# A mixture-of-experts router with its tokens on partitions, the centroid products as eight more columns of its weight, and the squared norm on ScalarE

## The chip, the cores and the metric

The kernel runs on one core of a Trainium2 chip. The metric is the device time of one execution in microseconds (us), and the median of several runs stands for a kernel. TensorE (PE in the profile) multiplies matrices, VectorE (DVE), ScalarE (ACT) and GpSimd (POOL) work element by element, SyncE (SP) issues most transfers. Each engine works through its own instructions in order and waits on semaphores where it needs another engine's result. Matrix products land in PSUM, everything else lives in SBUF.

## The reference, cut to what matters

Two layers, each an attention block and a feed-forward block, on x of 8 batches x 112 tokens x 256 features, with a context of 375 rows per batch, all in fp32:

```python
x = x + xattn0(layernorm(x), ctx)      # 16 heads of 16, 375 keys
x = x + moe(layernorm(x))              # 8 experts, the nearest 2 per token, hidden 1024
x = x + xattn1(layernorm(x), ctx, mask)
x = x + ffn1(layernorm(x))             # quantized linear, conv over tokens, silu, linear
```

The change is in the router of `moe`, which finds the two nearest of eight centroids c by a hyperbolic distance:

```python
xh   = project(x @ Wp + bp)            # project: x * min(1, 0.95 / |x|)
cp   = project(centroids)              # 8 x 256
xn   = min(sum(xh * xh), 0.99);  cn = min(sum(cp * cp), 0.99)
dot  = einsum("bnd,ed->bne", xh, cp)
diff = max(xn + cn - 2 * dot, 0)
dist = arccosh(max(1 + 2 * diff / ((1 - xn) * (1 - cn) + 1e-7), 1 + 1e-7))
top_v, top_i = top_k(-dist, 2);  weights = softmax(top_v)
```

So of the mapped token `y = x @ Wp + bp` the router needs just nine numbers: its squared norm and its product with each of the eight projected centroids. The factor min(1, 0.95/|y|) is applied to these afterwards.

## The kernel before, in words

**Attention of layer 0, 0 to about 280 us.** It goes by blocks of one batch b (112 tokens). A plan holds tuples (slot, place, step); the steps are issued in the order of slot and place, so work of several batches is interleaved by hand, and each engine keeps that order apart from what the program's scheduler moves where no dependence holds it. Batch b has slots 4b to 4b+12:

- `norm` and `query` (slots 4b-5, 4b-3): layer norm, turned by TensorE (t_n), then the q products (t_q, L534) of 16 instructions;
- `key` in two halves (t_k, L229; 8 instructions of 375 columns each) and `value` (t_v, L236; on DVE three additions put the bias onto v), both ahead of their use;
- `scores` for group g of four heads (slot 4b+g, place 0): four products (sc, L584) into two tiles, of which DVE takes the negative maximum of each row (top, L587), two instructions per group, 64 in layer 0;
- `lower` (slot 4b+4): turns the maxima (t_top, L603) and adds them to q (qa, L607);
- `turned` (slots 4b+5 to 4b+8): the scores again, with keys on partitions (t_p, L617), and exp on ACT (L629);
- `weighted` (one slot after): the products with v, collected in po (L639);
- `finish_o`, `finish_t`, `project` (slots 4b+10 to 4b+12): po copied by ACT, turned (t_o), divided by the sum of exp on DVE (o), turned again (t_oT), multiplied with the output weight (t_out), added to x, and the layer norm's statistics of the result on DVE.

PSUM is short: t_k, t_v, sc and t_p share three tiles of two banks ("pair"), and all of t_n, t_q, t_top, t_o, t_oT, t_out, t_rn, t_xh share one single bank (`misc`, buffer "m"). po has a bank, and behind its 448 columns the same bank has four slots of 16 columns (`small`) for the router's little products; the profile names these after the bank, so a router product is shown as `po`.

**The router.** `route(b, i)` has slot 4b+13+i, after the attention of its batch, so its steps lie between the steps of the next batches:

- step 0, `norm` and `turn`: rn on DVE, two transposes (t_rn, L288), a copy on ACT (rnT, L290), 128 features x 112 tokens twice;
- step 1, `hyper`: eight products t_xh (L297) with the features of the result on partitions, then four activations on ACT that add the bias: xh (L304) and its square xsq (L305), for each half of the features;
- step 2, `centre`: products with the centroids (L313, 8 columns) and of xsq with ones (L315, 1 column), which bring the tokens onto partitions; DVE copies the nine numbers (g, L317), clamps the squared norm (cx, L259) and works out 0.95/|y| by a bit trick and three Newton steps of tiny operations;
- step 3, `distance`: 11 operations of 112x1 or 112x8 on DVE;
- steps 4 and 5, `pick`: the two nearest, 9 small DVE operations and one sum;
- step 6, `place` (place 5 of its slot, the other steps 7): products with a lower triangle and ones count how many tokens came before (L364, L366); DVE reads the rank (row, L368) and forms row numbers (rf, at, L373); two indirect transfers on POOL (L375) scatter rn to the experts' lists in DRAM (`tok`). rn has two buffers, so rn of block b+2 waits for both scatters of block b;
- step 7, `weigh`: the two weights, on DVE.

`centroids()` (slot -1, place 7) projects the centroids once: a product with ones, and ten or so small DVE operations giving cproj, cn and cn1. In slots 8 to 19, at place 5, lie twelve steps that turn layer 1's two feed-forward weights into ternary values on DVE: `ternary` (absolute sums, L446, 1.2 us each, and others).

**From 297 us on.** Behind the last scatter, `further` works out which 13 further tiles of 128 tokens the experts need, then the experts' 21 tiles run (t_h L799, t_y L810), to about 520 us; layer 1 follows.

**Loads.** At the start SP issues x, the context, then the router's weight wp (L119), then w1T and w2T (1 MB each) for `ternary`, then the masks and zeros for the scratch in DRAM. ACT's queue issues the columns of biases, wq, wk, wv, `rows` (two biases of 256 values, broadcast to all partitions, L100) and wo.

Of the kernel before, what the change touches and what calls it, by code (L numbers as in the profile page):

```python
# [24 lines left out]
E, F = 8, 1024  # L25
# [29 lines left out]
def xattn_ffn_kernel(  # L55
# [190 lines left out]
    class Router:  # L246
        def __init__(self, pool, misc, small):
# [2 lines left out]
            self.cn = const([128, E], "cn")  # L250
            self.cn1 = const([128, E], "cn1")

        def tmp(self, name, n, p=S):
            return self.pool.tile([p, n], F32, tag=f"r_{name}", name=name)

# [7 lines left out]
        def centroids(self):  # L263

            cent = col("cent", 0, 2 * E).rearrange("p (c e) -> p c e", c=2)
            csq = self.pool.tile([128, 2, E], F32, tag="r_csq", name="csq")
            nc.vector.tensor_mul(csq, cent, cent)
            t = self.small("t_c")[:, :E]
            for c in range(2):
                nc.tensor.matmul(t, ones, csq[:, c, :], start=(c == 0), stop=(c == 1))  # L270
            nc.vector.tensor_copy(self.cn, t)
            cs = self.tmp("cs", E, 128)
            self.ball_scale(self.cn, cs, E, "c")
            nc.vector.tensor_mul(self.cproj, cent, cs.unsqueeze(1).to_broadcast([128, 2, E]))
            nc.vector.tensor_mul(self.cn, self.cn, cs)
            nc.vector.tensor_mul(self.cn, self.cn, cs)
            nc.vector.tensor_scalar_min(self.cn, self.cn, 0.99)
            nc.vector.tensor_scalar(self.cn1, self.cn, -1.0, 1.0, ALU.mult, ALU.add)

        def norm(self, b, stats):  # L280
            n = self.pool.tile([S, D], F32, tag="r_n", name="rn")
# [9 lines left out]
            return nT  # L291

        def hyper(self, nT):
            t = self.misc("t_xh")[:, : 2 * S].rearrange("p (c s) -> p c s", c=2)
            for o in range(2):
                for c in range(2):
                    nc.tensor.matmul(  # L297
                        t[:, o, :], wp_t[:, c, o * 128 : (o + 1) * 128], nT[:, c, :],
                        start=(c == 0), stop=(c == 1),
                    )  # L300
            xh = self.pool.tile([128, 2, S], F32, tag="r_xh", name="xh")
            xsq = self.pool.tile([128, 2, S], F32, tag="r_xsq", name="xsq")
            for o in range(2):
                nc.scalar.activation(xh[:, o, :], t[:, o, :], AF.Identity, bias=col("bp", o))  # L304
                nc.scalar.activation(xsq[:, o, :], t[:, o, :], AF.Square, bias=col("bp", o))  # L305
            return xh, xsq

        def centre(self, xh, xsq):

            tmp = self.tmp  # L310
            t = self.small("t_g")[:S, : E + 1]
            for c in range(2):
                nc.tensor.matmul(t[:, 0:E], xh[:, c, :], self.cproj[:, c, :], start=(c == 0), stop=(c == 1))  # L313
            for c in range(2):
                nc.tensor.matmul(t[:, E : E + 1], xsq[:, c, :], ones[:, 0:1], start=(c == 0), stop=(c == 1))  # L315
            g, r = tmp("g", E + 1), tmp("r", 1)
            nc.vector.tensor_copy(g, t)  # L317
            self.ball_scale(g[:, E : E + 1], r, 1, "x")
            return g, r

        def distance(self, g, r):

            tmp = self.tmp
            xn = tmp("xn", 1)
            nc.vector.scalar_tensor_tensor(xn, g[:, E : E + 1], r, r, ALU.mult, ALU.mult)
# [7 lines left out]
            nc.vector.scalar_tensor_tensor(dif, g[:, 0:E], m2r, self.cn[:S], ALU.mult, ALU.add)  # L333
# [145 lines left out]
    def attention(layer, stats, stats_next):  # L479
        scale = (0.25, 0.0625)[layer]  # L480
        res = None
        with (
# [219 lines left out]
            if layer == 0:  # L702
                rt = Router(ap, misc, small)
                rs = [{} for _ in range(B)]

                def route(b, step):
                    r = rs[b]
                    if step == 0:
                        r["n"] = rt.norm(b, stats_next.pop(b))
                        r["nT"] = rt.turn(r["n"])  # L710
                    elif step == 1:
                        r["x"] = rt.hyper(r.pop("nT"))
                    elif step == 2:
                        r["g"] = rt.centre(*r.pop("x"))
# [12 lines left out]
                add(-1, 7, rt.centroids)  # L727
                for i, step in enumerate(ternary(small)):
                    add(8 + i, 5, step)
                for b in range(B):  # L730
                    for i in range(8):
                        add(4 * b + 13 + i, 5 if i == 6 else 7, route, b, i)
                last = 4 * (B - 1)
                add(last - 2, 9, load_layer1, "kvq")
                add(last + 12, 9, load_layer1, "o")
                for b, ns in enumerate(((3, 6, 9), (15, 16, 17))):
                    add(last + ns[0], 4, key, 1, b, 0)
                    add(last + ns[1], 4, key, 1, b, 1)
                    add(last + ns[2], 4, value, 1, b)
# [288 lines left out]
```

## Time and the profile before

| | us |
|---|---|
| median of five runs | 793.2 |
| the five runs | 791.57, 792.49, 793.2, 793.35, 798.0 |
| the profiled execution, its own time | 793.08 |
| its span in the trace | 791.4 |

The profile is of that one execution; the span is what lies between its first and its last recorded instruction. Over the span TensorE is busy 672.4 us (85%), DVE 461.3 (58%), ACT 240.7 (30%), POOL 43.2 (5%), and the mean granted TensorE clock is 0.84 of full speed. By stretches of the run:

| stretch, us | what runs | PE busy | DVE busy | ACT busy | PE clock |
|---|---|---|---|---|---|
| 0 to 25 | loads, norms, centroids | 14.34 | 19.92 | 4.06 | 1.00 |
| 25 to 95 | attention of layer 0, no router yet | 68.19 | 45.55 | 20.31 | 0.95 |
| 95 to 265 | attention with the router between | 158.33 | 105.79 | 55.84 | 0.86 |
| 265 to 297 | the last blocks and the router's tail | 15.00 | 22.78 | 4.41 | 0.74 |
| 297 to 520 | experts | 211.52 | 61.78 | 73.17 | 0.89 |
| 520 to 791 | layer 1 | 205.03 | 205.52 | 82.88 | 0.76 |

In a line of the timeline the columns are: start (us), busy time, engine, line, operation, output<-inputs, tile (partitions x elements), and how many neighbouring instructions are put together; a bracket at the end gives how long the engine had waited just before, and for what. A matrix product's tile is shown as rows*columns of the weight and then rows x columns of its output. The router's t_xh of blocks 0 to 7 starts at 106.07, 133.84, 164.91, about 194.9, 217.87, 249.50, 266.81 and 276.36 us.

### The profile page before, as it was taken

The page shows a single profiled execution, that of the slowest core. Times are in us where ns is not written, and L with a number is a line of the kernel's source. Part 1 is how long each engine was busy: PE and PEld are TensorE (multiplying, and loading weights), DVE is VectorE, ACT ScalarE, POOL GpSimd, SP SyncE. Part 2 cuts the span into 40 slices and gives each one's busy share as a digit, 9 for nine tenths or more (in the row PEclk, how much of TensorE's full clock was granted, in tenths as well). Part 3 has the DMA queues.
Part 4 walks back from the last instruction along what each step waited for, and adds up shares of the span by engine and source line. Part 5 has one row for each costly group of instructions (what it writes and reads, how often), then busy time and mean ns, then how long its engine had stood idle before and what let it go on. Part 6 is the DMA issues. An engine that isn't in the chain of part 4 may idle for free.

```text
span 791.4 us, 15060 instructions
## 1 busy us (share of the span) xinstructions
PE 672.4 (85%) x5906; PEld 483.9 (61%) x5906; DVE 461.3 (58%) x1664; ACT 240.7 (30%) x476; POOL 43.2 (5%) x83
## 2 busy tenths in 40 slices
PE   4999998999999819999999959999999999845143
PEld 2666666666666518999999845666666656621033
DVE  8845667756834761111111048758987785469975
ACT  1124343224233204334343310223334322317300
POOL 4000000100000110000000061000000000000000
PEclk9999999789777959999999985579999975556558
DMA  9999101002000014987999420000000000000001
GB/s 302 368 345 329 62 2 54 14 13 68 14 13 7 32 35 176 343 316 282 357 344 358 185 75 26 1 2 1 3 1 2 2 2 1 1 1 0 0 11 35
DMA packets 37074, 82.73 MB, mean 105 GB/s; under 512 B 3228, under 2 KB 29196, under 8 KB 31628
## 3 DMA queue, kind: packets, MB, share of 16 engines
q1 hardware_dynamic: 34092, 76.25, 27.0%
q0 software_dynamic: 1536, 3.67, 1.5%
q10 hardware_dynamic: 1376, 1.87, 0.8%
q8 instruction: 46, 0.75, 0.4%
q14 instruction: 24, 0.20, 0.1%
HBM read 61.59 MB, written 20.19 MB: 103 GB/s over the span
## 4 chain that ended last, share of the span: by engine, by line
PE 70%; DVE 17%; DMA 5%; issue 4%; ACT 2%; SPq 0%; POOL 0%; ACTq 0%; DVEq 0%; POOLq 0%
PE t_k L229 11%; PE t_h L799 10%; PE t_y L810 9%; PE t_p L617 8%; PE sc L584 8%; PE po L639 6%; PE t_q L534 4%; PE t_v L236 4%; DMA tok<-rn,at 2%; PE t_out L672 2%; DVE am L924 2%; PE t_o L651 1%; DVE top L587 1%; PE t_y L942 1%; DVE y L913 1%
## 5 line engine op out<-in xcount | busy, mean ns | idle before, releaser
L229 PE MATMUL t_k<-ctx,wk 128*128 128x375 f32 x256 | 103.1, 550 | 4.3 <-DMA ctx<-in_ctxT_dram 3.5
L584 PE MATMUL sc<-k,q 16*112 16x375 f32 x512 | 87.7, 587 | 4.9 <-DVE pT L627 2.8
L799 PE MATMUL t_h<-tnT,we 128*128 128x128 f32 x672 | 91.5, 280 | 0.1
L799 PEld LDWEIGHTS t_h<-tnT,we 128*128 128x128 f32 x672 | 87.3, 193 | 6.5 <-ACT hT L803 1.6
L803 ACT ACTIVATE hT<-t_h,we 128x128 f32<-128x128 f32 x168 | 61.4, 367 | 90.7 <-PE t_h L799 85.1
L617 PE MATMUL t_p<-qa,k 17*125 17x112 f32 x1536 | 81.8, 324 | 2.3 <-DVE top L587 1.5
L810 PE MATMUL t_y<-we,hT 128*128 128x256 f32 x336 | 82.8, 380 | 0.0
L629 ACT ACTIVATE pT<-pT 125x672 f32<-125x672 f32 x64 | 48.8, 763 | 108.1 <-DVE pT L627 106.0
L617 PEld LDWEIGHTS t_p<-qa,k 17*125 17x125 f32 x1536 | 65.0, 217 | 21.2 <-issue 14.6
L229 PEld LDWEIGHTS t_k<-ctx,wk 128*128 128x128 f32 x256 | 52.2, 215 | 38.4 <-issue 11.5
L587 DVE TENSOR_REDUCE top<-sc 112x2 f32<-112x750 f32 x64 | 57.9, 934 | 27.8 <-PE sc L584 27.8
L627 DVE TENSOR_TENSOR pT<-t_p,maskT 125x336 f32<-125x336 f32 x128 | 56.6, 500 | 25.3 <-PE t_p L617 25.3
L639 PE MATMUL po<-pT,v 125*32 125x112 f32 x1536 | 66.3, 301 | 5.9 <-ACT pT L629 3.7
L629 ACT ACTIVATE pT<-t_p 125x672 f32<-125x672 f32 x64 | 43.3, 728 | 90.1 <-PE t_p L617 90.1
L594 DVE CUSTOM_DVE_ANT_0 sm<-sc,mask 112x375 f32<-112x375 f32 x128 | 63.0, 542 | 9.8 <-PE sc L584 9.7
L639 PEld LDWEIGHTS po<-pT,v 125*32 125x32 f32 x1536 | 43.9, 125 | 31.8 <-ACT pT L629 13.2
L810 PEld LDWEIGHTS t_y<-we,hT 128*128 128x128 f32 x336 | 59.1, 191 | 5.5
L788 DVE COPY tnT<-t_tn 128x256 f32<-128x256 f32 x21 | 8.9, 425 | 76.5 <-PE t_tn L786 70.2
L812 DVE TENSOR_TENSOR y<-t_y,we 128x256 f32<-128x256 f32 x21 | 8.9, 425 | 68.9 <-PE t_y L810 68.9
L584 PEld LDWEIGHTS sc<-k,q 16*112 16x112 f32 x512 | 29.4, 190 | 31.0 <-issue 18.9
L236 PE MATMUL t_v<-wv,ctx 128*125 128x256 f32 x192 | 45.9, 387 | 0.3 <-ACT k L557 0.3
L236 PEld LDWEIGHTS t_v<-wv,ctx 128*125 128x125 f32 x192 | 34.7, 187 | 7.4 <-ACT k L557 0.9
(207 smaller groups left out, 779.4 us busy)
## 6 DMA issues: line engine op xcount, KB each, us to landing
we<-in_WB_dram SPq DMA_DIRECT2D x21, 1152.0 KB, 8.0
we<-in_WA_dram SPq DMA_DIRECT2D x21, 1028.0 KB, 6.3
tok<-zero SPq DMA_DIRECT2D x8, 896.0 KB, 9.8
ysc<-zero SPq DMA_DIRECT2D x8, 896.0 KB, 11.1
ctx<-in_ctxT_dram SPq DMA_DIRECT2D x8, 375.0 KB, 7.6
tn<-tok SPq DMA_DIRECT2D x21, 128.0 KB, 7.0
ysc<-y SPq DMA_DIRECT2D x21, 128.0 KB, 3.2
we<-in_w1T_dram SPq DMA_DIRECT2D x1, 1024.0 KB, 9.0
```

What stands on the lines that cost most here:

```text
L229: nc.tensor.matmul(t, wts[layer]["k"][:, c, g * 128 : (g + 1) * 128], ctx_t[b][:, c, :], start=(c == 0), stop=(c == 1),)
L236: nc.tensor.matmul(t, ctx_t[b][:, c, i * KC : (i + 1) * KC], wts[layer]["v"][:, c, :], start=(c == 0), stop=(c == 1),)
L584: nc.tensor.matmul(ts[j // 2][:S, j % 2, :SK], q[r, g, :], k[r, g, :], start=True, stop=True)
L587: nc.vector.tensor_reduce(top[:, g, 2 * m : 2 * m + 2, A : A + 1], ts[m][:S, :, :SK], AX.X, ALU.max, negate=True,)
L594: nc.vector.tensor_tensor_reduce(out=sm, in0=ts[m][:S, i, :SK], in1=mask_t, scale=-1.0, scalar=3.0e38, op0=ALU.add, op1=ALU.min, accum_out ...
L617: nc.tensor.matmul(ts[j // 2][:KC, j % 2, c * S : (c + 1) * S], k[r, g, c * KC : (c + 1) * KC], qa[r, g, :], start=True, stop=True,)
L627: nc.vector.tensor_tensor(pT[:, i, :], src[:, i, :], maskT_t, ALU.add)
L629: nc.scalar.activation(pT, src, AF.Exp)
L639: nc.tensor.matmul(po[32 * j : 32 * j + 32, g, :], v[:, c, 4 * g + j, :], pTs[j // 2][:, j % 2, c * S : (c + 1) * S], start=(c == 0), stop ...
L799: nc.tensor.matmul(ph[:, i, :], w1[:, c, f * 128 : (f + 1) * 128], nt[:, c, :], start=(c == 0), stop=(c == 1),)
L803: nc.scalar.activation(hT[:, f, :], ph[:, i, :], AF.Gelu, bias=b1[:, f : f + 1])
L810: nc.tensor.matmul(py, hT[:, f, :], w2[:, f, :], start=(f == 0), stop=(f == NF - 1))
```

## The change

The mapped token is now made with the tokens on partitions: rnT is the stationary operand and the weight the moving one, so that t_xh is 112 tokens x 264 columns, 256 features and eight more columns that are the products with the projected centroids. It takes two products, issued as four instructions for fp32, instead of eight. DVE adds the bias row (256 values and eight more), ACT squares the 256 features and sums them along the row in the same instruction (`accum_out`). The products with the centroids and with ones, the four activations and the copy g are gone; `distance` reads the eight products from the new tile x, and cx reads the sum that ACT left.

For this `centroids()` multiplies Wp and the bias with the projected centroids once: four transposes of Wp, two copies by ACT, a broadcast copy of the bias, six products (twelve instructions), three copies by DVE. SP issues one transfer more, the bias row broadcast to 128 partitions (128 KB), right after wp; the input `rows` is longer by these 256 values. The steps' slots and places are the same as before.

```diff
     rowt = const([128, 2 * D], "rows")
-    nc.scalar.dma_start(out=rowt, in_=rows.partition_broadcast(128))
+    nc.scalar.dma_start(out=rowt, in_=rows[: 2 * D].partition_broadcast(128))
...
-    wp_t = load_w(wp, "wp", nc.sync)
+    wpc, bpc = const([128, 2, D + E], "wpc"), const([128, D + E], "bpc")
+    nc.sync.dma_start(out=wpc[:, :, :D], in_=wp.rearrange("(c p) n -> p c n", p=128))
+    nc.sync.dma_start(out=bpc[:, :D], in_=rows[2 * D :].partition_broadcast(128))
...
         def centroids(self):
...
+            wt = self.pool.tile([128, 2, D], F32, tag="r_wt", name="wpT")
+            for o in range(2):
+                t = self.misc("t_wp")[:, :D]
+                for c in range(2):
+                    nc.tensor.transpose(
+                        t[:, c * 128 : (c + 1) * 128], self.wpc[:, c, o * 128 : (o + 1) * 128], ident
+                    )
+                nc.scalar.copy(wt[:, o, :], t)
+            bw = self.pool.tile([128, 2, 128], F32, tag="r_bw", name="bpw")
+            nc.vector.tensor_copy(bw, col("bp", 0, 2).unsqueeze(2).to_broadcast([128, 2, 128]))
+            for k in range(3):
+                t = self.small("t_wc")[:, :E]
+                for o in range(2):
+                    lhs = wt[:, o, k * 128 : (k + 1) * 128] if k < 2 else bw[:, o, :]
+                    nc.tensor.matmul(t, lhs, self.cproj[:, o, :], start=(o == 0), stop=(o == 1))
+                nc.vector.tensor_copy(self.wpc[:, k, D:] if k < 2 else self.bpc[:, D:], t)
...
         def hyper(self, nT):
-            t = self.misc("t_xh")[:, : 2 * S].rearrange("p (c s) -> p c s", c=2)
-            for o in range(2):
-                for c in range(2):
-                    nc.tensor.matmul(
-                        t[:, o, :], wp_t[:, c, o * 128 : (o + 1) * 128], nT[:, c, :],
-                        start=(c == 0), stop=(c == 1),
-                    )
-            xh = self.pool.tile([128, 2, S], F32, tag="r_xh", name="xh")
-            xsq = self.pool.tile([128, 2, S], F32, tag="r_xsq", name="xsq")
-            for o in range(2):
-                nc.scalar.activation(xh[:, o, :], t[:, o, :], AF.Identity, bias=col("bp", o))
-                nc.scalar.activation(xsq[:, o, :], t[:, o, :], AF.Square, bias=col("bp", o))
-            return xh, xsq
-
-        def centre(self, xh, xsq):
-
-            tmp = self.tmp
-            t = self.small("t_g")[:S, : E + 1]
+
+            t = self.misc("t_xh")[:S, : D + E]
             for c in range(2):
-                nc.tensor.matmul(t[:, 0:E], xh[:, c, :], self.cproj[:, c, :], start=(c == 0), stop=(c == 1))
-            for c in range(2):
-                nc.tensor.matmul(t[:, E : E + 1], xsq[:, c, :], ones[:, 0:1], start=(c == 0), stop=(c == 1))
-            g, r = tmp("g", E + 1), tmp("r", 1)
-            nc.vector.tensor_copy(g, t)
-            self.ball_scale(g[:, E : E + 1], r, 1, "x")
-            return g, r
-
-        def distance(self, g, r):
+                nc.tensor.matmul(t, nT[:, c, :], self.wpc[:, c, :], start=(c == 0), stop=(c == 1))
+            x = self.pool.tile([S, D + E], F32, tag="r_x", name="xh")
+            nc.vector.tensor_tensor(x, t, self.bpc[:S], ALU.add)
+            return x
+
+        def centre(self, x):
+
+            g, r, sq = self.tmp("g", 1), self.tmp("r", 1), self.tmp("xsq", D)
+            nc.scalar.activation(sq, x[:, 0:D], AF.Square, accum_out=g)
+            self.ball_scale(g, r, 1, "x")
+            return x[:, D : D + E], g, r
```

More of the change, by code (lines that the diff above doesn't have):

```diff
@@ L251, in __init__ @@
             self.cn1 = const([128, E], "cn1")
+            self.wpc, self.bpc = wpc, bpc
         def tmp(self, name, n, p=S):
@@ L293, in hyper, with distance @@
         def hyper(self, nT):
[L294 to L321 removed]
+            t = self.misc("t_xh")[:S, : D + E]
+            for c in range(2):
+                nc.tensor.matmul(t, nT[:, c, :], self.wpc[:, c, :], start=(c == 0), stop=(c == 1))
[7 more added lines that the diff above has]
+            return x[:, D : D + E], g, r
+        def distance(self, dot, g, r):
             tmp = self.tmp
             xn = tmp("xn", 1)
[L325 removed]
+            nc.vector.scalar_tensor_tensor(xn, g, r, r, ALU.mult, ALU.mult)
             nc.vector.tensor_scalar_min(xn, xn, 0.99)
@@ L332, in distance @@
             dif = tmp("dif", E)
-            nc.vector.scalar_tensor_tensor(dif, g[:, 0:E], m2r, self.cn[:S], ALU.mult, ALU.add)
+            nc.vector.scalar_tensor_tensor(dif, dot, m2r, self.cn[:S], ALU.mult, ALU.add)
             nc.vector.tensor_scalar(dif, dif, xn, 0.0, ALU.add, ALU.max)
@@ L713, in route @@
                     elif step == 2:
-                        r["g"] = rt.centre(*r.pop("x"))
+                        r["g"] = rt.centre(r.pop("x"))
                     elif step == 3:
@@ L989 @@
         ),
-        "rows": np.concatenate([i["L0_xattn_b_kv"][D:], i["L0_xattn_b_out"]]),
+        "rows": np.concatenate([i["L0_xattn_b_kv"][D:], i["L0_xattn_b_out"], i["L0_ffn_bp"]]),
         "wq0": apart(i["L0_xattn_w_q"]),
```

## The prediction

> **What bounds the kernel now.** I read the page first: the chain of work that ended last, and the clock row of the 40 slices.
>
> ```profile
> PEclk9999999789777959999999985579999975556558
> ...
> PE 70%; DVE 17%; DMA 5%; issue 4%; ACT 2%; SPq 0%; POOL 0%; ACTq 0%; DVEq 0%; POOLq 0%
> ```
>
> TensorE holds 70% of the chain, and its clock falls in the eighth to thirteenth slice (139 to 257 us, 7 to 9 tenths), where the router runs. The change lies before 300 us; the router's results gate the experts there, so what it moves in that stretch passes on to the end. Next I read the timeline around block 1's router steps.
>
> ```profile
> 133.84 1.04 PE L297 MATMUL t_xh<-rnT,wp 128*128 128x112 f32 x8
> 134.91 0.35 ACT L304 ACTIVATE xh<-t_xh,cols 128x112 f32<-128x112 f32 x1 [2.25 <-PE t_xh L297]
> ...
> 135.74 1.79 DVE L587 TENSOR_REDUCE top<-sc 112x2 f32<-112x750 f32 x2 [0.62 <-PE sc L584]
> 136.06 0.41 PE L663 MATMUL t_oT<-ident,o 112*128 112x112 f32 x2 [0.35 <-ACT xsq L305]
> ...
> 139.31 0.56 PE L313 MATMUL po<-cproj,xh 128*112 128x8 f32 x4
> 139.72 0.53 PE L315 MATMUL po<-ones,xsq 128*112 128x1 f32 x4
> 140.18 1.60 PE L584 MATMUL sc<-k,q 16*112 16x375 f32 x6
> ...
> 146.52 4.72 PE L229 MATMUL t_k<-ctx,wk 128*128 128x375 f32 x8
> ...
> 151.67 0.62 DVE L607 TENSOR_TENSOR qa<-t_top,q 128x448 f32<-128x448 f32 x1 [0.91 <-PE t_top L603]
> ...
> 153.10 2.04 PE L534 MATMUL t_q<-nT,wq 128*128 128x112 f32 x16
> ```
>
> To see there: L313 and L315 hold TensorE for 0.87 us (139.31 to 140.18) though they stream 8 columns and 1; xsq (L305) holds the one "m" buffer, so t_oT waits 0.35; and qa waits 0.91 for TensorE, so in this block TensorE is the late one. In block 0, at full clock, it was the other way: TensorE waited 2.21 us up to 121.05 for DVE. Windows of 1 us show why: the clock is 1.00 in 139 to 140, 0.61 in 140 to 141, 0.50 to 150, 0.77 in 150 to 151. It was half from 140.2 to 150.5, and likewise 170.9 to 177.8, 201.7 to 205.1, 211.9 to 229.0 and 239.2 to 249.4. Last I read the late blocks and the tail.
>
> ```profile
> 231.30 0.16 DVE L373 CAST at<-rf 112x2 int32<-112x2 f32 x1
> ...
> 237.93 0.41 DVE L217 TENSOR_SCALAR rn<-x,mv,rs 112x256 f32<-112x256 f32 x1 [1.30 <-DMA tok<-rn,at]
> ```
>
> ```profile
> 275.46 0.41 PE L288 MATMUL t_rn<-ident,rn 112*128 112x112 f32 x2
> 276.36 1.15 PE L297 MATMUL t_xh<-rnT,wp 128*128 128x112 f32 x8 [0.49 <-ACT rnT L290]
> ...
> 280.40 0.15 DVE L259 TENSOR_SCALAR cx<-g 112x1 f32<-112x1 f32 x1
> ```
>
> From 230 us on, a block's two scatters (from 231.30 on, behind at) gate the rn of the block two later, whose buffer they still read. Block 7's chain is serial from t_rn to the end of layer 0.
>
> **The change, part by part.** The order is that of the changed kernel's instructions on each engine, the durations are the trace's.
>
> *Prices per block.* t_xh: 8 instructions of 112 columns, 0.97 us apart (133.84 to 134.81), become 4 of 264; t_v streams 256 in 0.23 (12 in 2.79), so 0.95: nothing gained. L313 and L315 go: -0.87 at full clock, 1.3 at half (170.58 to 171.87). ACT loses four activations, 0.35 each and 0.25 apart (1.1 us, from 134.91 to 136.00), and gains a Square of 256 elements. Its summed output no row shows; ends are the 224-element copy (0.35) and the 672-element exponential (0.73), I take 0.45, near the first by size. DVE loses the copy g (0.17) and gains an add of 112x264 out of PSUM; L571's 125x256 took 0.42, so 0.43. DVE's first clamp (cx) now waits for ACT's Square, behind the add.
>
> The Trainium skill, "ScalarE: Activation LUTs" (What ACT_TABLE_LOAD costs), gives 186 ns + 0.833 ns an element for an ACTIVATE without pointer operands: 0.40 for this Square, an estimate. By it the sum below would be 0.2 lower; no run here shows the summed output.
>
> *Start: +2.2.* centroids() gains four transposes, two ACT copies, six products and four DVE copies, and SP a transfer of 128 KB. wp was issued at 14.99 and took 6.9 us (21.9); its first reader comes after t_n (24.19 to 24.55), so 3 us cover it. The extra transfer moves w1T and w2T back one place each on SP: w1T goes at 16.11, not 15.40, and lands near 25.2 (9.0 us). On DVE the first L446 sum (1.21) now stands ahead of the first maximum, which before began at 25.77: the sum runs 25.8 to 27.0, the maximum to 27.9, the copy of the first new column to 28.0. The second pair of products waits for that copy (same PSUM bank), so TensorE, in order, has t_k's rest only then: 28.1 + 0.4 (products) + 1.35 (half of t_k) + 0.4 + 0.65, then both scores 0.75: t_q at 31.75 against 29.55. Later waits up to 95 us are on DVE and ACT (1.2 us in all), none on a transfer, so the 2.2 passes on. Bounds: 0 if the gaps take it, 3.5 if every copy adds its own wait.
>
> *Blocks 0 to 3: -3.2.* Block 1 replayed at full clock. v adds end at 135.13, add 135.56, Square 136.08, cx 136.25, the two maxima end at 137.1 and 138.25 (before 136.65 and 137.53). t_oT starts 0.35 earlier, but t_p's second half waits for the first maximum and gives it back. Next, 16 serial small operations of norm and distance (0.2 to 0.25 each by the tail's rows: 3.0 us) run before the rank's row read, which now is at 141.2; po waits for that read. Eleven more (1.6 us) stand before the next maximum: it ends at 143.85, the second at 145.0, and t_k starts at 145.05. Without L313 and L315 the scores were ready at 139.25, so this wait is the new one: behind it in DVE's queue are x, the layer norm and qa, and t_p, t_k and t_top on TensorE. The old order at full clock gives t_k at 143.5. But the old order then has 46 small operations before qa, 6.8 us from x (143.96 to 150.75), the new 35, 4.45 us: t_q waits for qa, at 150.1 new against 150.45 old, so -0.4 for block 0. In the half-clock blocks TensorE is last: t_k at 145.0 instead of 146.52, and t_q 0.9 earlier (block 1), 1.0 (block 2, t_k 176.15 instead of 178.01, then qa late), 0.9 taken for block 3.
>
> *Blocks 4 to 7 and the tail: -2.5.* at (231.30) no longer waits for g (231.22): -0.4, and rn with it, since two scatters take 6.6 us from at to rn; at 254.85 waited the same way from rf's end 254.21: -0.5. Between t_rn of block 6 and x of block 7, L313, L315 and the waits for xh and xsq (0.40, 0.24) go and the wait for the add comes: -1.1. From t_rn(7) to cx took 4.94; new: t_xh ends 1.97 after t_rn, add 0.53, Square 0.55, then the v copy (0.95) that now stands between, 4.4: -0.5.
>
> Sum: 2.2 - 3.2 - 2.5 = -3.5. The profiled execution took 793.08 (its span and 1.7 us around it), 0.1 under the median of 793.2: 789.6.
>
> The clock is a rule to weigh. The trace lost it at 140.2 with TensorE never idle, in a stretch of thin products (po, t_p, L364, L313, L315), and kept it through 119 to 121, when TensorE was idle. The Trainium skill, "TensorE: Matmul & The Clock Gate" (The HAM clock gate), has the gate fall after an idle window of about 3.4 us. The stretches agree with windows of 3.4 (10.2, 6.8, 3.4, 17.1, 10.2 us long), the idleness does not. By the page's rule the change, which opens no such gap, would leave the clock, and the sum, as they are.
>
> **Rivals.**
> - *The clock stays up in blocks 1 to 3.* For: thin products leave the windows that lost it. Against: the waits before t_k lengthen a stretch without wide products from 8.7 to 10.3 us. Then t_xh to t_q takes 16.25 everywhere, against 19.26, 18.12 and some 17.7: -3.0 - 1.9 - 1.5 - 0.4 = -6.8 in place of -3.2: 786.0.
> - *The blocks gain nothing*, DVE being the bound and the cx wait costing what qa's shorter queue gives. For: 121.05, where TensorE waited for DVE. Against: qa's 0.91 wait in block 1. 2.2 - 2.5: 792.8.
> - *Slower: the 28 operations put between the maxima hold t_k, and it is not given back.* Place: row read and second maximum, t_k 1.55 later in each of four blocks. It decides once qa is ready before TensorE comes to t_q. For: qa waited for TensorE at 151.67. Against: at half clock old t_k was later still (146.52). 2.2 + 6.2 - 2.5: 799.0.
>
> **How the numbers follow.** Forecast 0.40 (its own range 787.5 to 791.5), clock 0.14, no gain 0.20, slower 0.26: block 0 shows DVE already the late engine at full clock, and three of the four early blocks are only in part at half. The range leaves out the lower half of the clock case (786.0, so from 785.0, as some of it will keep a window) and the slower case from above its value of 799.0, so to 799.5, together 0.2. It takes in 789.6 with eight Squares at their upper bound (8 x 0.28 = 2.2) and the start at 3.5. Half a per cent, about what a measurement of this kernel can tell from no change, is at 789.2 and 797.2: faster is the clock case and over half of the forecast, 0.37; same the rest and no gain, 0.37; slower 0.26.
>
> **What would show it.** No t_g products; 32 t_xh instructions near 0.45 to 0.5 us; Square near 0.45; the second t_q near 31.75 instead of 29.55; cx behind Square; x of a block later than its second maximum, qa some 4.5 us after x; t_rn(7) to cx 4.4. Half-clock windows counted from 95 to 265 us (47.7 us now) decide between forecast and clock case; t_k starts against t_q starts decide the slower one. The prediction is wrong if the clock's stretches move by more than one window of 3.4 us, or if Square takes over 0.73.

## The result, and the profile after

The changed kernel takes 796.75 us in the median, the kernel before 794.34 over the runs taken beside it: a ratio of 1.0029, with a 95% interval of 1.0018 to 1.0039. It is 2.3 us slower (1.4 to 3.1), where 3.5 less was forecast. The range of 785.0 to 799.5 holds the time; the direction was wrong.

The profiled execution took 793.79 (span 792.1), 3.0 under the median of its kernel; that of before took 793.08, 1.3 under its own. So the two traces are only 0.7 apart, and what follows from them is where the time moved; the 2.3 comes from the timed runs. The page of the changed kernel has, as answers to the lines shown of before:

```profile
span 792.1 us, 14880 instructions
...
PEclk9999998999767958999999985579999985556558
...
PE 66%; DVE 18%; DMA 8%; issue 4%; ACT 2%; SPq 1%; POOL 0%; DVEq 0%; POOLq 0%; ACTq 0%
```

The clock falls as often as before, but elsewhere: the seventh slice (119 to 139 us) has 8 instead of 9, the twelfth 6 instead of 7, and the eighth and ninth 9 instead of 7 and 8. TensorE's share of the chain is lower (66%, 70 before), DVE's and the transfers' higher. Following the same work through both traces:

| from, to | before | after | difference |
|---|---|---|---|
| start to t_xh of block 0 | 106.07 | 110.36 | +4.29 |
| t_xh of block 0 to t_xh of block 1 | 27.77 | 30.83 | +3.06 |
| blocks 1 to 2, 2 to 3, 3 to 4 | 31.07, 29.93, 23.03 | 28.55, 27.97, 24.75 | -2.52, -1.96, +1.72 |
| t_xh of block 4 to cx of block 7 | 62.53 | 57.66 | -4.87 |
| cx of block 7 to the first t_h | 17.86 | 17.61 | -0.25 |
| first t_h to the end of the span | 493.1 | 494.3 | +1.2 |

One thing has to be taken off the first row: the first t_q, which runs before anything that the fold (the products of Wp and the bias with the centroids) adds on TensorE, starts at 18.49 instead of 19.81, and in the experiments anywhere from 18.58 to 20.73. Counted from it, t_xh of block 0 is 5.6 later, not 4.3.

Up to the experts the changed kernel is 0.5 ahead in this execution. The 1.2 behind them lie in no line that the change touches; the page has t_h waiting 1.1 for an expert's weights, and none such before.

**The start.** TensorE's timeline of the kernel before, up to the second t_q (columns as before):

```profile
24.47 0.90 PE L584 MATMUL sc<-k,q 16*112 16x375 f32 x8
25.64 2.76 PE L229 MATMUL t_k<-ctx,wk 128*128 128x375 f32 x8 [0.27 <-PE sc L584]
28.33 1.29 PE L584 MATMUL sc<-k,q 16*112 16x375 f32 x8
29.55 2.04 PE L534 MATMUL t_q<-nT,wq 128*128 128x112 f32 x16
```

The same of the changed kernel, from 23.36 to the last scores ahead of the second t_q, which starts at 33.90:

```profile
23.36 0.88 PE L592 MATMUL sc<-k,q 16*112 16x375 f32 x2
24.17 0.44 PE L287 MATMUL t_wp<-ident,wpc 128*128 128x128 f32 x2
24.54 0.88 PE L592 MATMUL sc<-k,q 16*112 16x375 f32 x2
25.35 0.44 PE L287 MATMUL t_wp<-ident,wpc 128*128 128x128 f32 x2
25.63 0.29 PE L297 MATMUL po<-cproj,wpT 128*128 128x8 f32 x2
25.84 0.88 PE L592 MATMUL sc<-k,q 16*112 16x375 f32 x2
26.65 0.39 PE L297 MATMUL po<-cproj,wpT 128*128 128x8 f32 x2
26.97 0.88 PE L592 MATMUL sc<-k,q 16*112 16x375 f32 x2
27.78 1.15 PE L231 MATMUL t_k<-ctx,wk 128*128 128x375 f32 x2
...
33.07 0.90 PE L592 MATMUL sc<-k,q 16*112 16x375 f32 x8
```

A group of scores is four heads of two instructions, each on 16 of the array's 128 rows. In one piece the eight take 0.83 us (33.07 to the t_q at 33.90): the heads run at once. Here the fold's transposes and products stand between the heads, and each head takes 0.81 by itself, so that from 23.36 to 27.78 pass 4.42 us, against 1.17 before (24.47 to 25.64): 3.24 for the four heads, 1.18 for the fold's instructions between them. The Trainium skill, "TensorE: Matmul & The Clock Gate" (Part 3: Packing small matmuls — row/col tiling), says that products on different strips of 32 rows overlap in the array; both traces agree for heads that are neighbours in the instruction stream. With instructions of the full array between them, the lines above show no such overlap.

TensorE did not wait for the fold's copies here: it is busy in all 14.00 us from 20 to 34, and on DVE each of the three copies waits for its product (0.50, 0.79 and 1.53).

And the clock fell behind this thin stretch, though TensorE had work in it all the time. Two stretches of the kernel before (columns: window, its length, busy time and instructions of PE, PEld, DVE, ACT and POOL, then the granted clock, the DMA share and GB/s), and the same two of the changed kernel:

```profile
28.00:33.00 5.00, 5.00 (x31) 3.39 (x30) 5.00 (x6) 1.04 (x2) 0.00 (x0) 1.00 1.08 378
118.00:130.00 12.00, 9.53 (x113) 6.18 (x116) 11.48 (x42) 3.69 (x8) 0.00 (x0) 1.00 0.14 43
```

```profile
28.00:33.00 5.00, 5.00 (x16) 3.14 (x15) 2.67 (x5) 0.00 (x0) 0.00 (x0) 0.66 1.07 370
118.00:130.00 12.00, 9.92 (x75) 6.38 (x76) 10.25 (x54) 2.87 (x5) 0.72 (x1) 0.72 0.01 3
```

From 29.43 the t_k instructions are 0.63 apart instead of 0.31. The changed kernel and the four kernels below that have the heads apart all show their first half clock at 28 to 31 us; of the kernel before and the eight others below none shows half clock ahead of 41 us.

**Block 0.** Two lines of TensorE's timeline in block 0 of the kernel before:

```profile
114.67 2.79 PE L229 MATMUL t_k<-ctx,wk 128*128 128x375 f32 x8
121.05 0.78 PE L639 MATMUL po<-pT,v 125*32 125x112 f32 x24 [2.21 <-DVE w1mean L455]
```

The timeline of DVE, ACT and TensorE in block 0's router of the changed kernel:

```profile
111.57 0.42 DVE L319 TENSOR_TENSOR xh<-t_xh,bpc 112x264 f32<-112x264 f32 x1
112.02 0.42 ACT L325 ACTIVATE xsq<-xh 112x256 f32<-112x256 f32 x1 [2.84 <-DVE xh L319]
112.34 0.19 ACT L325 ACTIVATION_READ_ACCUMULATOR xsq<-xh 112x1 f32 x1
112.56 0.15 DVE L263 TENSOR_SCALAR cx<-g 112x1 f32<-112x1 f32 x1 [0.58 <-ACT xsq L325]
...
117.86 0.47 PE L625 MATMUL t_p<-qa,k 17*125 17x112 f32 x4
...
119.42 0.93 DVE L595 TENSOR_REDUCE top<-sc 112x2 f32<-112x750 f32 x1
...
120.41 1.59 PE L625 MATMUL t_p<-qa,k 17*125 17x112 f32 x20 [2.08 <-DVE top L595]
...
121.93 5.37 PE L231 MATMUL t_k<-ctx,wk 128*128 128x375 f32 x8
```

The Square costs what was taken for it (0.42; 0.45 taken), with a second ACT instruction of 0.19 behind it that reads the sum. The new wait is further down: DVE works through norm, distance and the first pick before it takes the maximum at 119.42. t_p waits 2.08 for that, and the t_k behind it runs at half clock, 5.37 instead of 2.79. That the wait brought the half clock is not shown: the kernel before waited 2.21 up to 121.05, and its clock stayed at 1.00 from 118 to 130.

The early blocks as a whole follow the clock. Its mean over blocks 0 to 3 (from t_xh to the next t_xh) was 1.00, 0.84, 0.89 and 0.80 before, and is 0.89, 0.94, 1.00 and 0.73 now. If what is missing to 1.00 is lost time (an estimate; where TensorE waits it costs nothing), that makes +3.4, -3.3, -3.3 and +2.1 us, close to the measured +3.06, -2.52, -1.96 and +1.72. Without it blocks 0 to 3 gain nothing. Blocks 4 to 7 gain their 4.87 at the same clock, 0.83 before and 0.82 now.

**The tail** got better, as forecast. From t_rn of block 7 to its cx passed 4.94 before, now 3.99:

```profile
276.13 0.41 PE L308 MATMUL t_rn<-ident,rn 112*128 112x112 f32 x2 [0.27 <-DVE rn L219]
...
277.04 1.15 PE L317 MATMUL t_xh<-wpc,rnT 128*112 128x264 f32 x4
...
280.12 0.14 DVE L263 TENSOR_SCALAR cx<-g 112x1 f32<-112x1 f32 x1
```

### The profile page after: what moved, and what is told of

The parts are those of the page before. It is cut to its first block, busy times and chain, and to the rows that moved or that the text cites. A ratio compares the mean times of both kernels' runs of the same rounds, so it can differ in the third digit from the quotient of the medians.

```text
span 792.1 us, 14880 instructions
## 1 busy us (share of the span) xinstructions
PE 668.5 (84%) x5826; PEld 476.7 (60%) x5826; DVE 463.4 (59%) x1668; ACT 236.9 (30%) x462; POOL 43.2 (5%) x83
## 4 chain that ended last, share of the span: by engine, by line
PE 66%; DVE 18%; DMA 8%; issue 4%; ACT 2%; SPq 1%; POOL 0%; DVEq 0%; POOLq 0%; ACTq 0%
PE t_k L231 11%; PE t_h L807 9%; PE t_y L818 8%; PE t_p L625 8%; PE sc L592 7%; PE po L647 6%; PE t_q L542 5%; PE t_v L238 4%; DMA tok<-rn,at 4%; DMA we<-in_WA_dram 2%; DVE top L595 2%; DVE am L932 2%; PE t_out L680 2%; PE t_o L659 1%; PE t_y L950 1%
## 5 line engine op out<-in xcount | busy, mean ns | idle before, releaser
L625 PE MATMUL t_p<-qa,k 17*125 17x112 f32 x1536 | 84.7, 324 | 7.7 <-DVE top L595 5.5
L625 PEld LDWEIGHTS t_p<-qa,k 17*125 17x125 f32 x1536 | 66.7, 215 | 27.1 <-issue 14.1
```

The costliest lines, as they stand in the source:

```text
L625: nc.tensor.matmul(ts[j // 2][:KC, j % 2, c * S : (c + 1) * S], k[r, g, c * KC : (c + 1) * KC], qa[r, g, :], start=True, stop=True,)
```

## The experiments

Ratios are to the kernel before, run beside it on the same chip, with 95% intervals; absolute times differ by some us from chip to chip. Line numbers in a fence are those of that kernel.

### The two halves of the change, each by itself

The fold alone, in the kernel before:

```diff
-    wp_t = load_w(wp, "wp", nc.sync)
+    wpc, bpc = const([128, 2, D + E], "wpc"), const([128, D + E], "bpc")
+    nc.sync.dma_start(out=wpc[:, :, :D], in_=wp.rearrange("(c p) n -> p c n", p=128))
+    nc.sync.dma_start(out=bpc[:, :D], in_=rows[2 * D :].partition_broadcast(128))
+    wp_t = wpc
...
         def centroids(self):
+            wt = self.pool.tile([128, 2, D], F32, tag="r_wt", name="wpT")
...
```

> The kernel before, with only the start of the change: the bias row is loaded and Wp and the bias are multiplied with the centroids, but the router goes on as before and nothing reads the eight columns. Theory A (the start is the whole loss: the three copies of the products wait on DVE behind the score maxima and the 1.21 us sums, and TensorE waits for them): the second t_q starts at 33.9 as in the changed kernel (29.55 before), everything to 95 us is 4.3 later, and the time is 3.0 to 4.5 above the kernel before. Theory B (what is lost at the start is taken in later, the loss is in the router's blocks): the second t_q is late too, but the time is within 1 us of the kernel before.

Measured: 1.0072 (1.0046 to 1.0098), 5.7 us slower. The second t_q starts at 37.5 and t_xh of block 0 at 113.94, so it starts even later than in the changed kernel (its first t_q, ahead of the fold, is 2.2 later too). From t_xh of block 0 to that of block 4 it takes 112.9, about the 111.8 of before: nothing is taken in later. Theory A names the right place, with too small a size, and its cause, the copies, is tried below; B falls.

The change without the fold:

```diff
-            wt = self.pool.tile([128, 2, D], F32, tag="r_wt", name="wpT")
...
+            nc.vector.tensor_copy(self.wpc[:, :, D:], self.wpc[:, :, 0:E])
+            nc.vector.tensor_copy(self.bpc[:, D:], self.bpc[:, 0:E])
```

> The changed kernel without the fold at the start: the eight columns are copies of the first eight columns of Wp and of the bias, so tokens go to other experts than in the reference (the number of tiles stays the same). The rest, the bias row's load too, is as in the changed kernel. Theory A: the second t_q is back near 29.6, block 0's order on DVE is as bad as in the changed kernel, and the time is 1.5 to 2.5 below the kernel before (the change's 2.4 less the start's 4.3). Theory B: 1 to 2.5 above the kernel before.

Measured: 0.9940 (0.9912 to 0.9967), 4.8 us faster. The second t_q is at 29.16. Blocks 0 to 4 take 111.6 and block 0 is as slow as in the changed kernel (30.83); from t_xh of block 4 to cx of block 7 it takes 58.5 (62.5 before). So the router's rework gains about 5 (2.6 to 7.0), more than theory A gave, and the start gives all of it back. The extra transfer is in this kernel too, and costs nothing that shows.

### What the start loses: the copies, or TensorE's order?

```diff
-                nc.vector.tensor_copy(self.wpc[:, k, D:] if k < 2 else self.bpc[:, D:], t)
+                nc.scalar.copy(self.wpc[:, k, D:] if k < 2 else self.bpc[:, D:], t)
```

> The changed kernel with the three copies of the folded products on ACT instead of DVE. Theory A (the loss at the start is the place in DVE's queue): the second t_q starts 2.0 to 3.0 earlier than in the changed kernel, near 31.3, and the time falls by the same against the changed kernel, to about the kernel before (-0.6 to +0.4). Rival (TensorE's own time for the transposes and the thin products is the loss): the second t_q moves by less than 1, and the time stays 2 above the kernel before.

Measured: 1.0020 (0.9995 to 1.0046); the second t_q at 34.26. The copies wait for nothing but their products now, and the start is no earlier. TensorE's timeline of this kernel:

```profile
27.32 0.88 PE L592 MATMUL sc<-k,q 16*112 16x375 f32 x2
...
29.76 3.73 PE L231 MATMUL t_k<-ctx,wk 128*128 128x375 f32 x6
33.42 0.90 PE L592 MATMUL sc<-k,q 16*112 16x375 f32 x8
34.26 0.92 PE L542 MATMUL t_q<-nT,wq 128*128 128x112 f32 x6
```

The heads are still apart (0.88 for a head's two instructions), and six t_k instructions take 3.66 (0.31 each would be 1.9). So the copies' place in DVE's queue was not the loss at the second t_q, and the rival is at least half right: it is TensorE's time. Is it the fold's own work, or where it lies? The next kernel holds the first two groups together by issue order alone (no waits), and lets one copy read all 24 columns (heads[0] is the last score product traced, and then the fold's last product):

```diff
+                def fold():
+                    with tc.issue_after(heads[0]):
+                        heads[0] = rt.fold()
+                add(0, 1, fold)
...
+                if layer == 0 and step == scores and args == (0, 1):
+                    with tc.issue_after(heads[0]):
+                        step(*args)
...
-                nc.vector.tensor_copy(self.wpc[:, k, D:] if k < 2 else self.bpc[:, D:], t)
+            nc.vector.tensor_copy(wall[:, :, D:], tw.rearrange("p (k e) -> p k e", k=3))
```

> The changed kernel with the fold's place on TensorE repaired by issue order: its transposes and products come between the first two groups of score products, inside t_k, and no longer between the four heads of one group; the 24 new columns lie in one PSUM tile and one DVE copy reads them. Theory D (the start's loss is TensorE's: with the fold's full-array instructions between the heads of the first group, the heads no longer run at once, 4.4 us from 23.36 to 27.78 against 1.17 before, and the thin stretch costs half clock in the t_k behind it): the second t_q starts between 30.5 and 32 instead of 33.9, the half clock of 28 to 32 is gone or shorter, and the time is 2 to 4 below the changed kernel, 0 to 1.7 below the kernel before. Rival (the fold's own work on TensorE is the loss, wherever it lies): second t_q over 33 and no gain against the changed kernel's +0.3%.

Measured: 0.9932 (0.9907 to 0.9958), 5.4 us faster than before. TensorE's timeline:

```profile
24.08 0.90 PE L599 MATMUL sc<-k,q 16*112 16x375 f32 x8
24.91 0.44 PE L290 MATMUL t_wp<-ident,wpc 128*128 128x128 f32 x2
25.20 0.90 PE L232 MATMUL t_k<-ctx,wk 128*128 128x375 f32 x2
...
29.48 0.90 PE L599 MATMUL sc<-k,q 16*112 16x375 f32 x8
30.31 0.92 PE L549 MATMUL t_q<-nT,wq 128*128 128x112 f32 x6
```

The same transposes and products, and the second t_q is at 30.31, 0.8 after that of before. The half clock of 28 to 32 is gone, and another at 45 to 49 with it, so that t_xh of block 0 comes at 105.14, 5.2 earlier than in the changed kernel. The gain is more than theory D gave (0 to 1.7 below the kernel before). This edit did two things, so the order was then tried with the three copies left on DVE:

```diff
-            nc.vector.tensor_copy(wall[:, :, D:], tw.rearrange("p (k e) -> p k e", k=3))
+                nc.vector.tensor_copy(self.wpc[:, k, D:] if k < 2 else self.bpc[:, D:], t)
```

> The run with the fold between whole groups changed two things at once: the groups' heads stay together, and one copy takes the place of three. Here the heads stay together by the same issue order, and the three separate copies on DVE are kept. Theory D (the split heads and the half clock behind them are the loss at the start, not the copies): the last t_q product of batch 1 and the t_top of batch 0 come within 1.5 us of where the run with one copy has them, and the time is 1.5 to 5 below the kernel before. Rival (the copies' place in DVE's queue is the loss): t_top of batch 0 is 3 us or more later than in the run with one copy, and the time is 0 to 3 above the kernel before.

Measured: 0.9980 (0.9954 to 1.0006). t_top of batch 0 is at 45.66 (49.69 in the changed kernel, 44.44 with one copy, 45.37 before). Keeping the heads together brings 4.03 of the 5.25, the single copy the other 1.22; by the trace theory D holds, and its rival, which had t_top 3 us or more behind the run with one copy, falls. In time the kernel is 1.6 below the kernel before (3.7 below to 0.5 above), at the lower edge of what D gave. Against the changed kernel the order alone brings 3.9 (1.7 to 6.1 by the two intervals), and the single copy, run on another chip, another 3.8 (0.9 to 6.7), more than the 1.2 at t_top. In the traces blocks 0 to 4 took 115.0 (111.6 with one copy), with 58.0 us at half clock between 95 and 265 us (51.2). Why they did is open.

### What the blocks lose: DVE's order

In the program the distance stands behind the maxima; the scheduler moved it ahead. One edit puts it behind them (latest[0] is the last maximum traced):

```diff
+                if layer == 0 and step == route and args[1] in (3,):
+                    with tc.issue_after(latest[0]):
+                        step(*args)
```

> The changed kernel with one edit: on DVE the distance step of a block is issued behind the score maxima that its slot's scores need (issue order alone, no wait), so the 28 small operations no longer stand between them in blocks 0 to 3. Theory C (these hold t_p and t_k, and in block 0 the 2.08 us wait costs the clock too): in block 0 the wait of t_p is gone, t_k starts some 2 us earlier from t_xh than in the changed kernel (11.6), the time from t_xh of block 0 to that of block 1 falls from 30.8 to about 28, and the time is 1.5 to 3 below the changed kernel. Rival (the blocks' time is set by the half clock, whose windows come anyway, or by the whole of DVE's queue before qa): t_xh of block 0 to that of block 1 stays over 30, and the time is within 1 us of the changed kernel.

Measured: 1.0053 (1.0026 to 1.0081), slower than the changed kernel. In the trace block 0 does what theory C says: t_p's wait is gone, and block 0 to block 1 takes 27.44 (30.83). (The clock still falls once in it, to a mean of 0.57 from 118 to 122, with TensorE busy all the time, so this fall had no wait ahead of it.) But block 1 to 2 takes 32.98 instead of 28.55. The timeline of TensorE and DVE in block 1 of this kernel:

```profile
148.19 2.79 PE L231 MATMUL t_k<-ctx,wk 128*128 128x375 f32 x8
...
155.88 0.62 DVE L615 TENSOR_TENSOR qa<-t_top,q 128x448 f32<-128x448 f32 x1
...
156.55 0.77 PE L542 MATMUL t_q<-nT,wq 128*128 128x112 f32 x2 [3.65 <-DVE qa L615]
```

t_k is early (8.4 after t_xh, 10.8 in the changed kernel), at full clock, and then t_q waits 3.65 for qa: distance, picks and most of the weights now stand in one row before qa, DVE itself waits 1.06 in it for block 0's scatters (at rn, L219), and at half clock behind the wait t_q takes 3.8 instead of 2.0. What counts here is the whole queue up to qa. So the picks were moved behind the maxima of their slots as well:

```diff
-                if layer == 0 and step == route and args[1] in (3,):
+                if layer == 0 and step == route and args[1] in (3, 4, 5):
```

> The changed kernel with the distance step and both pick steps each issued on DVE behind the score maxima of their slot (the run before this moved the distance alone: its 13 operations and the picks then stood in one piece ahead of qa, and t_q waited 3.65 us for qa in block 1). Here only distance and the first pick stand ahead of qa. Theory E (what costs is the length of DVE's queue from x to qa, and the wait for it takes TensorE's clock): t_q of block 1 no longer waits for qa over 1 us, blocks 0 to 3 (t_xh of block 0 to that of block 4) take less than the 112.1 of the changed kernel, by 2 to 5, and the time is 1 to 4 below the changed kernel. Rival (the later placement makes rn of the next blocks and the scatters late): the gain is lost between t_xh of blocks 4 and 7 (54.5 in the changed kernel).

Measured: 0.9918 (0.9886 to 0.9950). The start is as bad as ever (second t_q at 35.39), but t_q of block 1 no longer waits, blocks 0 to 4 take 106.0 instead of 112.1, and block 4 to the last cx 57.1 (57.7), so theory E holds, with more than it gave (6.1 in the blocks, and by the two ratios 8.8 in time), and its rival falls. Both edits together:

> Both edits in one kernel. If theories D and E hold, the second t_q starts near 31, t_xh of blocks 0 to 4 takes under 110, and the time is 3 to 7 below the changed kernel, 1 to 5 below the kernel before (ratio 0.994 to 0.999). If only D holds, as the run with D's edit alone.

Measured: 0.9829 (0.9788 to 0.9871), 13.6 us faster than before, more than the 1 to 5 that was expected: blocks 0 to 4 in 104.2, the experts' first t_h at 286.3 (298.3 before). A milder pair, the distance late in block 0 alone:

```diff
-                elif layer == 0 and step == route and True and args[1] in (3, 4, 5):
+                elif layer == 0 and step == route and args[0] == 0 and args[1] in (3,):
```

> D's edit, and the distance late in block 0 alone, where it took 3.4 us from t_xh of block 0 to that of block 1 (30.8 to 27.4); the other blocks keep the changed kernel's order. Theory D with block 0's order: second t_q near 31, 27 to 28 from block 0 to block 1, time 3 to 6 below the changed kernel. Rival (the half-clock windows come back in the next block, as the clock takes away what the order gives): block 1 to block 2 takes over 30 (28.5 in the changed kernel) and the time is as in the run with D's edit alone.

Measured: 0.9901 (0.9865 to 0.9937), not to be told from the fold's edit alone (0.9932). Block 0 to 1 takes 27.45, block 1 to 2 27.88, so the rival's idea that the clock takes it back at once does not show, though its forecast of the time holds.

Does that order belong to the change? The same three steps, issued late in the kernel before, with nothing of the change:

> The kernel before with the issue order alone that helped the changed kernel (distance and picks behind their slot's score maxima; nothing of the change). Theory F (DVE's queue ahead of qa was a loss of the kernel before as well, so the gain of the late picks is not the change's): 2 to 5 below the kernel before (0.994 to 0.9975), and t_q of blocks 1 to 3 comes earlier from t_xh than 19.3, 18.1 and 17.7 us. Rival (it only mends what the change's own order spoiled): within 1 us of the kernel before.

Measured: 0.9918 (0.9897 to 0.9940), 6.5 us faster, more than theory F gave. In time theory F holds: DVE's order was a loss of the kernel before too. In the trace, of an execution 5.6 above its kernel's median, t_q comes 13.4 and 14.4 after t_xh in blocks 0 and 1 (15.9 and 19.3 before), but 19.4 in block 2 (18.1); behind block 3's t_xh there is no t_q in layer 0. Of the 1.7% that both edits bring over the kernel before, about 0.8 is DVE's order, and about 0.9 the change with its fold mended; taken in the other order it is 0.7 for the change (0.9932) and 1.0 for DVE's order.

### The parts of the router's rework

The eight thin instructions per block put back, unread, into the kernel with both edits:

```diff
+            t = self.small("t_g")[:S, : E + 1]
+            for c in range(2):
+                nc.tensor.matmul(t[:, 0:E], nT[:, c, :], self.cproj[:, c, :], start=(c == 0), stop=(c == 1))
+            for c in range(2):
+                nc.tensor.matmul(t[:, E : E + 1], nT[:, c, :], ones[:, 0:1], start=(c == 0), stop=(c == 1))
```

> The kernel with both edits, and on top eight thin instructions per block as in the kernel before, four of 8 columns and four of 1 column; their result is not read, so they cost TensorE and nothing else. This prices what the change takes off TensorE. The prediction's price is 0.87 at full clock and 1.3 at half, 7 to 10 us for 8 blocks where TensorE is last. Theory H (TensorE is the late engine in most blocks): 3 to 8 above the kernel with both edits. Rival (DVE is late, TensorE's 0.9 per block fits into its waits): under 2 above it.

Measured: 0.9975 (0.9950 to 1.0001) against 0.9829, on different chips: 11.6 us more (7.7 to 15.5 by the two intervals), above the 3 to 8 of theory H, and its rival falls. The instructions' own time in the trace is 0.7 to 1.5 a block, 8.2 in all, which is inside the interval. They also hold others; in block 5, TensorE's timeline of this kernel:

```profile
253.39 0.56 PE L333 MATMUL po<-cproj,rnT 128*112 128x8 f32 x4 [0.86 <-DVE row L386]
253.81 0.80 PE L335 MATMUL po<-ones,rnT 128*112 128x1 f32 x4
254.47 1.17 PE L694 MATMUL t_out<-wo,oT 128*112 128x256 f32 x2
```

They write the PSUM bank that DVE reads row from, so they wait for it (in blocks 1 and 3 too, 0.3 to 0.4), and hold t_out behind them; block 5 to 6 takes 20.6 instead of 15.3. And the half clock between 95 and 265 us adds up to 64.9 instead of 47.8. The run prices these instructions in this order alone; it is not the change's gain, since the changed kernel without the fold gains 4.8 in all.

The Square on DVE in place of ACT, in the kernel with both edits:

```diff
-            nc.scalar.activation(sq, x[:, 0:D], AF.Square, accum_out=g)
+            nc.vector.tensor_tensor_reduce(
+                out=sq, in0=x[:, 0:D], in1=x[:, 0:D], scale=1.0, scalar=0.0,
+                op0=ALU.mult, op1=ALU.add, accum_out=g,
+            )
```

> The kernel with both edits (fold between whole groups, picks late), and the squared norm on DVE, one multiply with a sum of 112x256, instead of ACT's Square. The trace of the changed kernel has the Square at 0.42 and a second ACT instruction of 0.19 that reads the sum, and cx starts 0.99 after the add's start plus 0.42; on DVE some 0.42 to 0.55 takes their place. Theory G (each block's chain and above all block 7's is shortened by the way to ACT and back): t_xh(7) to cx falls by 0.2 to 0.5, the time by 0.5 to 2 against the kernel with both edits (ratio to the kernel before 0.980 to 0.982). Rival (0.45 more in DVE's full queue per block costs as much): the same 0.983 within its interval, or above.

Measured: 0.9814 (0.9785 to 0.9844), which can't be told from 0.9829. In the trace cx follows 0.47 after the start of DVE's square, and t_rn to cx of block 7 falls from 3.98 to 3.10, more than expected, since the copy of v (0.95) no longer stands between. Within what these runs can tell, that ScalarE makes the norm is neither what the change gains by nor what it loses by.

## Why the prediction was wrong, point by point

- **Start, +2.2: the step that failed.** "28.1 + 0.4 (products) + 1.35 (half of t_k) + 0.4 + 0.65, then both scores 0.75: t_q at 31.75" (its terms add up to 31.65) took the copies' waits as the price, the score products as one piece, and full clock. The trace has 33.90. The first group's heads were taken apart by the fold (4.42 us from 23.36 to 27.78, 1.17 before), and the clock fell behind it. The changed kernel's order on TensorE, which the sum used for the waits, had the heads apart; it was not asked what that costs. The fold by itself costs 5.7 (3.7 to 7.8), not 2.2. The waits for copies that the sum priced are not in the changed kernel's trace, where each copy waits for TensorE; with the heads kept together, three copies instead of one cost 1.2 at t_top. That no later wait takes the loss in was right.
- **Blocks 0 to 3, -3.2:** +0.3 in the trace. Block 0 was given -0.4 and took +3.06: that the operations between the maxima make t_p and t_k late was in the text, but not that the clock would be lower there (0.72 from 118 to 130, 1.00 before). The late maxima are the mechanism of the slower rival, in one block of four. Blocks 1 and 2 gained 2.5 and 2.0, more than the 0.9 and 1.0 given, with less half clock: t_xh to t_q takes 16.7 and 16.2 there, near the 16.25 of the rival in which the clock stays up. Block 3 lost 1.7; its 0.9 was given for an earlier t_q, but the last t_q of layer 0 starts at 183.03, in block 2.
- **Blocks 4 to 7 and the tail, -2.5:** -4.9 in the trace. The tail's step was too small (-0.5; it is -0.95): its own terms, 1.97, 0.53, 0.55 and 0.95, add up to 4.0, not to the 4.4 that was written, and the trace has 3.99. The rest was too small as well.
- **The sum of the blocks** is then -4.6 in the trace, -4.8 by the kernel without the fold, against -5.7 forecast. That it comes out near is in part luck: the early blocks, which were to bring more than half of it, brought nothing, and the late ones twice their part.
- **The prices** of t_xh (0.97 to 0.98 for four), add (0.42) and Square (0.42) held. The estimate from the Trainium skill, "ScalarE: Activation LUTs" (What ACT_TABLE_LOAD costs), for the Square was 0.40 us; the summed output is an instruction of its own, 0.19, which neither had.
- **The clock:** half clock between 95 and 265 us adds up to 44.4, 47.8 before; the forecast that the sum stays held, within one window. But the stretches moved to other places, and one came at the start. By the rule of the Trainium skill, "TensorE: Matmul & The Clock Gate" (The HAM clock gate), an idle window, the stretch from 23.36 to 27.78 should have kept the clock, as TensorE had no gap in it; the trace decides against that. What does decide the clock is open.
- **Not explained in full:** the traces differ by 0.7, the timed runs by 2.3. Of the 1.6 between them, 1.3 is that TensorE's first t_q came 1.3 earlier in the changed kernel's profiled execution. Both kernels' single runs spread over 9 to 10 us; which windows of half clock a run gets would be a reason, but no run here shows it.

## What to carry to other kernels

In this kernel small products that share the array ran at once only as neighbours: before adding full-array work to a dense stretch of TensorE's queue, look in the order of instructions for groups that it would split, and price the split by the group's time per member. A one-time preparation was paid in full here, since TensorE had no later wait to take it in, and its place mattered: the same six products and four transposes cost 5.7 us in one place, and in another, with one copy behind them, nothing that can be measured (0.9932 with them, 0.9940 without); with three copies it was 0.9980. And a gain of DVE's order should be tried on the kernel before as well, else it is credited to the change.

## What was not expected of the hardware

- Four heads of 16 rows: 0.83 us for eight instructions in one piece, 0.81 for two by themselves.
- Half clock without any idle time of TensorE: after 4.4 us of thin instructions at the start, 0.66 from 28 to 33 us; with the heads together, no fall there. And the other way round, full clock kept through 2.21 us of idle time in block 0 of the kernel before.
- An ACT instruction with a summed output is two: 0.42 and 0.19 us.
- Thin products of 8 columns and 1 column, 8.2 us in eight blocks by the trace, were worth 11.6 us (7.7 to 15.5). Waits at their PSUM bank (0.86 in block 5) and more half clock (64.9 us instead of 47.8) stand beside them; whether these add to the cost was not told apart.
